# Shared experts and routers of two layers: from the half of the batch into each batch's own thread

## The chip, the cores and the metric

The kernel runs on one core of a Trainium2 chip. The metric is the device time of one execution in microseconds (us), lower is better. The core has five engines that run beside each other, each with its own queue of instructions in a fixed order: TensorE (matmuls; PE in the profile, with its weight loads as PEld), VectorE (DVE), ScalarE (ACT), GpSimd (POOL) and SyncE (SP, which here issues the loads by DMA). An instruction waits in its queue for everything that stands ahead of it, and for semaphores set by other engines or by DMAs.

## The reference, cut to what matters

The program is a decoder of four layers on x of shape [4 batches, 256 tokens, 128 features], in fp32. Each layer is three residual steps:

```python
x = x + attention(layernorm(x))
x = x + cross_attention(layernorm(x), context)
x = x + ffn(layernorm(x))
```

Two of the four FFNs are mixtures of experts with one **shared expert** that every token passes. Layer 0 (16 routed experts of 128 hidden features, each token goes to the best one; f is the layer's normalised input):

```python
logits = f @ router_w.T
score  = sigmoid(logits of the best expert)
routed = down[e](up[e](f * score) * silu(gate[e](f * score)))
shared = (silu(f @ shared_gate_w.T) * (f @ shared_up_w.T)) @ shared_down_w.T   # 512 hidden
ffn    = shared + routed
```

Layer 3 (7 routed experts of 512 hidden features, each token goes to the best two; the shared expert has 512 hidden features as well):

```python
probs = softmax(f @ router_w.T)
top_vals, top_idx = top_k(probs, 2)
top_vals = top_vals / (top_vals.sum(-1) + 1e-9)
routed = sum over the two of top_vals * swiglu[e](f)
ffn    = swiglu_shared(f) + routed
```

The other layers have attentions of several kinds. Two of their parts come up below: layer 3's attention over 64 slots of heads (`heads64`), and layer 3's cross-attention step, in which the 16 heads of one token attend to each other (`across_heads`), so that it consists of elementwise products and sums.

## The kernel before, in words

**Tiles of tokens.** The four batches are two halves: half 0 is batches 0 and 1, half 1 is batches 2 and 3. A batch has two tiles of 128 tokens (tokens on partitions), a half four. The residual x, the normalised y and its transpose yT (features on partitions, 512 tokens in the free dimension) are kept in SBUF for each half.

**Threads and a planner.** Every part of the network is a Python generator. It issues instructions until it needs something, and then yields that need: a tile that must be written, a buffer that must be free, a weight that must be in the ring, or a `Side` (a group of threads) that must be done. A planner, `Clock`, keeps an estimated time for every engine, tile and buffer while the program is built, and `Threads.run` always resumes the generator whose needs are met earliest by these estimates. So the order of the instructions in each engine's queue is written out while the program is built, and follows from the planner's estimates and from what waits for what; on the chip nothing is reordered. All engine calls go through one helper (`Timed`), so that nearly every row of the profile has line 480; rows are told apart by the names of their tiles.

**The halves.** `half(hf)` runs once for each half, both as threads beside each other. `part(hf, batches)` makes the generators, once for both batches of a half (n = 4 tiles of tokens) and once for each batch alone (n = 2):

```python
for head, _ in parts: side.start(head())     # per batch
yield side                                   # both batches done
yield from experts0()                        # layer 0's FFN, both batches together
for _, tail in parts: side.start(tail())     # per batch
yield side
yield from experts3()                        # layer 3's FFN
```

`head` is layer 0's attention (`retention`), cross-attention (`cross0`, tiles x0..) and `normalised`, which writes y and yT. `tail` is everything from layer 1 to layer 3's cross-attention: `linear`, `latent`, `experts1` (issued by batch 0 for all batches), `heads16` twice (tiles a2.., x2..), `ternary`, `heads64` (tiles h6..), `across_heads` and `normalised`.

**across_heads** of one batch does four products on GpSimd for the scores (tiles am, each followed by a sum `en<-am` on VectorE), a softmax (mx, exp on ScalarE, sums), four products on GpSimd for the output (tiles aw, summed on VectorE), a layernorm, transposes (azT), one product on TensorE (apo) and the residual sum. Then `normalised` writes y, and yT by the transposes yt on TensorE.

**The mixture FFN.** `experts0` and `experts3` work on a half's 512 tokens:

- `shared_expert(name)` loops over four groups of 128 hidden features: `gate_up` issues two matmuls of 512 columns (tile gu, gate and up), ScalarE copies the gate and takes a tanh, VectorE makes h in two steps; then a down matmul adds to `acc`. `add_half` scales `acc` on ScalarE, transposes it back (fT, four transposes) and adds it to x. In the trace a matmul in fp32 leaves two records.
- `routes0` and `routes3` are the routers: four small matmuls (lg, lg3), a chain of small VectorE instructions for the best experts and their weights (max, max_index for each tile), and then `dispatch`.
- `dispatch` compares each token's expert with 0, 1, 2, ... (tile mine), counts by two matmuls (rank), and works out on VectorE the place of every token in tiles of 128 tokens of one expert (room, count, end, place, and as integers placei). GpSimd then scatters the rows of y to these places in DRAM (an indirect DMA for each tile and choice: four in layer 0, eight in layer 3). At last the expert of each tile (ids) goes to `ring.numbers`, from which SyncE reads the addresses of the weights to load.
- `routed` loads the sorted tokens back (xs), transposes them (xsT, xT), and goes over 19 tiles in layer 0 (four to a step) or 14 in layer 3, with gate_up (gu, h), a product (eo), a scaled copy (eos) and a store to DRAM (results).
- `collected` gathers each token's rows from the results by indirect DMAs on GpSimd (tile got), and they are added to x.

In `experts0` the shared expert `L0F4` runs beside the router. In `experts3` the shared expert `L3F7` of half 0 runs beside its router, ahead of the routed tiles; that of half 1 is started after its routed tiles, beside the gathers of the results.

**The ring of weights.** `Ring` holds the weights of each half in three slots (`SLOTS`), filled by SyncE in one fixed order. The next name is loaded once the name three places ahead of it was given up by `ring.done`. In half 1 the order ends with the 14 routed weights L3G0 to L3G13 and then L3F7; five of the 14 have two slots of their own (tile late).

**What sets the order around the change.** Both halves share TensorE's PSUM buffers and all engines. Half 0 runs ahead; while GpSimd works on the `across_heads` of half 0, TensorE works on half 1's `heads64`, and so on. `h6p` is the softmax's scaling in `heads64`, on GpSimd.

## The time and the profile before

| | |
|---|---|
| median of 3 runs | 1201.03 us (1199.13 to 1206.34) |
| profiled execution | 1190.56 us, of which the profile's span is 1188.5 us |
| mean granted TensorE clock | 0.811 of full speed |
| instructions | 15677 |
| TensorE busy (PE) | 918.7 us, 77% of the span |
| weight loads (PEld) | 613.5 us, 52% |
| VectorE busy | 756.1 us, 64% |
| ScalarE busy | 385.7 us, 32% |
| GpSimd busy | 385.0 us, 32% |
| moved by DMA | 73.52 MB, 62 GB/s over the span |

How to read the lines that are shown below. The profile is of one execution. In the slices, each digit is the busy share of one of 40 equal parts of the span (29.7 us each) in tenths, 9 being 90% or more; PEclk is the granted TensorE clock in the same way. A row "by stretch" gives for a window of time each engine's busy time with the number of instructions in brackets, and then the granted clock, the busy share of the DMA engines and what they moved. A line of the chain of waits gives the start in us from the span's start, the duration in us, the engine, and the output tile, with the inputs behind an arrow; "x4" means that four instructions of one kind were folded into the line. The chain is followed back from the last instruction, at each step to what released it.

Where the stages of the end lie in this execution: `across_heads` of half 0 from 836 to 920 us, the routed tiles of half 0 and `heads64` of half 1 from 920 to 1025, `across_heads` of half 1 from 1025 to 1085, then its router, its dispatch, and its routed tiles from 1125 on.

### The profile page before, as it was taken

To read this page: it belongs to the slowest core of one execution; us is meant where nothing else is said; L and a number is where in the kernel's file an instruction comes from. 1 tells how busy PE (TensorE), PEld (TensorE's weight loads), DVE (VectorE), ACT (ScalarE), POOL (GpSimd) and SP (SyncE) were. 2 spreads that over 40 slices of the span, in tenths; PEclk is the share of its full clock that TensorE was granted. 3 is DMA by queue.
4 is the path that set the end of the run, shared out by engine and by line. 5 is a ranking of instruction groups with operands and counts; after the bars stand their busy time and mean duration, and the time that the engine had idled before them with its cause. 6 is when DMAs were issued, how large, how long until landed. Compare 5 with 4: busy or idle time off the path is not lost.

```text
span 1188.5 us, 15677 instructions
## 1 busy us (share of the span) xinstructions
PE 918.7 (77%) x5605; PEld 613.5 (52%) x5606; DVE 756.1 (64%) x1836; ACT 385.7 (32%) x870; POOL 385.0 (32%) x493
## 2 busy tenths in 40 slices
PE   2887978996776768999998879997278999732296
PEld 1654544573464446665655445655144567721194
DVE  4547547445785697566578658756877655675154
ACT  0222522352132122224562717363033354210043
POOL 3533031002224310133100535223866422574202
PEclk9989978697888675558795859999678999965599
DMA  9210100441523000001000210011000224411572
GB/s 302 70 55 5 37 1 18 113 127 36 175 65 109 28 0 28 1 1 52 1 1 6 73 45 1 1 46 54 18 1 1 71 77 141 147 35 27 182 235 89
DMA packets 43069, 73.52 MB, mean 62 GB/s; under 512 B 3696, under 2 KB 33008, under 8 KB 42992
## 3 DMA queue, kind: packets, MB, share of 16 engines
q1 hardware_dynamic: 31600, 61.90, 16.3%
q0 software_dynamic: 2560, 6.30, 1.7%
q10 hardware_dynamic: 8832, 4.33, 1.2%
q8 instruction: 44, 0.72, 0.3%
q14 instruction: 33, 0.27, 0.1%
HBM read 63.60 MB, written 8.91 MB: 61 GB/s over the span
## 4 chain that ended last, share of the span: by engine, by line
PE 55%; DVE 20%; POOL 12%; issue 5%; ACT 4%; DMA 3%; another core or an unknown queue 0%; SPq 0%; POOLq 0%; DVEq 0%; ACTq 0%
PE gu L480 7%; PE pj_b L480 6%; DVE mx_b L480 3%; POOL aw_b L480 3%; PE h6av_b L480 3%; PE lc_b L480 3%; POOL ri_b L480 3%; PE h6pt_b L480 2%; PE h6sc_b L480 2%; PE a2sa_b L480 2%; PE eo L480 2%; PE x2av_b L480 2%; PE x0av_b L480 2%; PE a2sb_b L480 2%; PE a2av_b L480 2%
## 5 line engine op out<-in xcount | busy, mean ns | idle before, releaser
L480 POOL TENSOR_TENSOR ri_b<-ri_b,mhalf 128x2 f32<-128x2 f32 (+2 forms) x69 | 58.0, 843 | 243.3 <-DVE ri_b L480 236.3
L480 POOL TENSOR_SCALAR h6p_b<-h6p_b,rec_b 128x256 f32<-128x256 f32 x128 | 59.3, 483 | 117.1 <-DVE rec_b L480 96.5
L480 ACT ACTIVATE h6p_b<-h6sc_b,nm_b 128x256 f32<-128x256 f32 x128 | 59.0, 475 | 56.4 <-DVE nm_b L480 54.0
L480 ACT COPY h<-gu 128x512 f32<-128x512 f32 (+1 forms) x54 | 31.4, 581 | 101.2 <-PE gu L480 101.0
L480 DVE TENSOR_TENSOR h<-h,gu 128x512 f32<-128x512 f32 (+1 forms) x54 | 36.6, 677 | 34.1 <-ACT sl L480 32.9
L480 POOL TENSOR_SCALAR_AFFINE_SELECT a2p_b<-a2p_b 128x256 f32<-128x256 f32 x64 | 27.2, 449 | 81.4 <-ACT a2p_b L480 81.4
L480 ACT COPY yT<-yt_b 128x256 f32<-128x256 f32 x31 | 11.5, 372 | 125.2 <-PE yt_b L480 125.2
L480 PE MATMUL lc_b<-w_L1X,luT 96*128 96x384 f32 x96 | 49.1, 648 | 2.9 <-DVE lpr_b L480 2.4
L480 PE MATMUL gu<-xT,w_L3G 128*128 128x128 f32 x368 | 49.9, 291 | 1.8 <-DMA w_L3G<-in_L3G_dram 1.5
L480 PE MATMUL h6pt_b<-ident,h6p_b 128*128 128x128 f32 x256 | 41.4, 288 | 10.3 <-POOL h6p_b L480 3.8
L480 PEld LDWEIGHTS gu<-xT,w_L3G 128*128 128x128 f32 x368 | 46.6, 204 | 4.9 <-issue 2.5
L480 POOL DMA_INDIRECT got<-results,placei x24 | 23.9, 994 | 77.9 <-PE gu L480 57.2
L480 POOL TENSOR_TENSOR aw_b<-en_b,as_b 128x1024 f32<-128x1024 f32 x16 | 45.5, 2876 | 8.7 <-DVE en_b L480 8.7
L480 PE MATMUL h6sc_b<-hkt_b,hqt_b 64*128 64x256 f32 x256 | 47.8, 434 | 0.1
L480 PE MATMUL yt_b<-ident,y 128*128 128x128 f32 x82 | 23.0, 366 | 31.7 <-DVE y L480 17.8
L480 DVE TENSOR_REDUCE mx_b<-x0sa_b 128x4 f32<-128x1024 f32 x32 | 38.7, 1220 | 12.7 <-PE x0sa_b L480 8.2
L480 PE MATMUL h6av_b<-h6pT_b,hv_b 128*64 128x256 f32 x256 | 46.0, 398 | 0.7 <-DVE h6pT_b L480 0.4
L480 DVE TENSOR_REDUCE nm_b<-h6sc_b 128x4 f32<-128x1024 f32 x32 | 38.9, 1217 | 10.2 <-PE h6sc_b L480 10.0
L480 DVE TENSOR_REDUCE mx_b<-x2sa_b 128x4 f32<-128x1024 f32 x32 | 38.8, 1218 | 8.1 <-PE x2sa_b L480 7.3
L480 PEld LDWEIGHTS h6pt_b<-ident,h6p_b 128*128 128x128 f32 x256 | 28.8, 144 | 27.0 <-issue 6.8
L480 POOL DMA_INDIRECT places<-y,placei x24 | 23.5, 979 | 58.1 <-DVE placei L480 52.0
L480 PE MATMUL a2sa_b<-a2k_b,a2q_b 32*128 32x256 f32 (+1 forms) x128 | 30.0, 458 | 13.7 <-DVE mx_b L480 11.4
(460 smaller groups left out, 2523.5 us busy)
## 6 DMA issues: line engine op xcount, KB each, us to landing
w_L3G<-in_L3G_dram SPq DMA_DIRECT2D x23, 768.0 KB, 6.3
w_L0G<-in_L0G_dram SPq DMA_DIRECT2D x38, 192.0 KB, 2.4
late<-in_L3G_dram SPq DMA_DIRECT2D x5, 768.0 KB, 4.7
xs<-places SPq DMA_DIRECT2D x6, 512.0 KB, 4.1
places<-ones SPq DMA_DIRECT2D x2, 1216.0 KB
results<-eos ACTq DMA_DIRECT2D x8, 256.0 KB, 4.1
results<-eos ACTq DMA_DIRECT2D x14, 128.0 KB, 3.0
w_L2A<-in_L2A_dram SPq DMA_DIRECT2D x2, 776.0 KB
```

The costliest lines, as they stand in the source:

```text
L480: return getattr(self.engine, op)(*args, **kw)
```

## The change

Each batch's thread now computes its own shared expert and its own router. A batch's `head` ends with the router `routes0` and the shared expert `L0F4`, its `tail` with `routes3` and `L3F7`. The two batches of a half share a `Routes` object, which holds the chosen experts (and in layer 3 the weights) of all four tiles and counts the batches that have written theirs. `experts0` and `experts3` of the half are left with the dispatch, the routed tiles, the gathers and the sum. They wait for the `Routes` to be complete and not for the batches' threads; `half` runs them ahead of `yield side`, so a shared expert may still be at work while the dispatch goes on.

In `shared_expert` a batch has 256 tokens: two calls of `gate_up`, each with two groups of 128 hidden features side by side (four matmuls of 256 columns, h again 512 wide), then the four down matmuls into an `acc` of 256 columns, the scaled copy, two transposes and the sum into x. The slot of the ring is given up when both batches are done. In half 1's ring L3F7 now stands ahead of L3G0. The final store of x moves from `experts3` to `half`.

```diff
     rings = [
         Ring(0, first_half + ["L3F7"] + routed3, []),
-        Ring(1, ["L1K"] + [n for n in first_half if n not in alone] + routed3 + ["L3F7"], [n for i, n in enumerate(routed3) if i % 5 > 2]),
+        Ring(1, ["L1K"] + [n for n in first_half if n not in alone] + ["L3F7"] + routed3, [n for i, n in enumerate(routed3) if i % 5 > 2]),
     ]
...
+    class Routes:
+        def __init__(self, name, experts, weights=None):
+            self.experts, self.done = const.tile(experts, F32, tag=f"{name}e", name=f"{name}e"), 0
+            if weights is not None:
+                self.weights = const.tile(weights, F32, tag=f"{name}w", name=f"{name}w")
+
+        def ready(self):
+            return clock.ready(self.experts) if self.done == 2 else math.inf
+
+    routing = [
+        {"L0G": Routes(f"L0G{hf}", [P, 4]), "L3G": Routes(f"L3G{hf}", [P, 2, 4], [P, 2, 4])} for hf in range(2)
+    ]
...
         def shared_expert(name):
-            yield ring.there(name), av_free
+            yield ring.there(name)
             w = ring[name]
-            acc = av_tile("acc")
             hs = []
...
-            for i in range(4):
+            for i in range(2):
                 yield sc_free, t2_free, h_free(i)
-                hs.append(gate_up(i, [(w["g"][:, i, :], w["u"][:, i, :], yT)]))
-                if i > 1:
-                    yield hs[i - 2][1]
-                    product(i - 2)
-            for i in (2, 3):
-                yield hs[i][1]
-                product(i)
-            ring.done(name)
-            yield from add_half(acc)
+                hs.append(gate_up(i, [(w["g"][:, j, :], w["u"][:, j, :], yT) for j in (2 * i, 2 * i + 1)]))
+            yield hs[0][1]
+            yield hs[1][1], av_free
+            acc = av_tile("acc", (P, S))
+            for j in range(4):
+                h = hs[j // 2][0][:, j % 2 * S : j % 2 * S + S]
+                pe.matmul(acc, w["d"][:, j, :], h, start=(j == 0), stop=(j == 3))
+            for h, _ in hs:
+                release(h)
+            ring.done(name, users=2)
+            yield t2_free
+            o = t2("fo", (P, S))
+            nc.scalar.mul(o, acc, 0.5)
+            yield o, ps_free
+            add(transposed(o.rearrange("p (t q) -> p t q", q=P), n, "fT").rearrange("p (t q) -> p t q", q=P))
...
         def experts0():
...
-            got = []
-            side.start(routes0(got))
-            yield from shared_expert("L0F4")
-            yield side
+            yield routes["L0G"].ready
+            placei = yield from dispatch("L0G", routes["L0G"].experts, 16, 16, TILES0)
             yield from routed("L0G", TILES0, 4, 1)
             yield results[hf]
-            t = collected(got[0])
+            t = collected(placei)
...
-        def routes0(got):
+        def routes0():
             yield ps_free
-            pl = ps("lg", (P, 4, 16))
-            for t in range(4):
+            pl = ps("lg", (P, n, 16))
+            for t in range(n):
                 pe.matmul(pl[:, t, :], yT[:, t * P : (t + 1) * P], wM["r0"], start=True, stop=True)
...
+            routes["L0G"].done += 1
...
         def experts3():
-            got = []
-            side.start(routes3(got))
-            if hf == 0:
-                yield from shared_expert("L3F7")
-            yield side
+            yield routes["L3G"].ready
+            experts, tv = routes["L3G"].experts, routes["L3G"].weights
+            placei = yield from dispatch("L3G", experts.rearrange("p j t -> p (j t)"), 8, 7, TILES3)
             yield from routed("L3G", TILES3, 1, 1 + hf)
-            if hf == 1:
-                side.start(shared_expert("L3F7"))
             yield results[hf]
-            t = collected(got[1])
+            t = collected(placei)
...
-            yield side
-            nc.sync.dma_start(out[2 * hf : 2 * hf + 2].rearrange("b (c p) d -> p (b c) d", p=P), x)
...
         def head():
...
             yield from cross0()
             yield from normalised()
+            side.start(routes0())
+            yield from shared_expert("L0F4")
+            yield side
 
         def tail():
...
             yield from across_heads()
             yield from normalised()
+            side.start(routes3())
+            yield from shared_expert("L3F7")
+            yield side
...
         for head, _ in parts:
             side.start(head())
+        yield from experts0()
         yield side
-        yield from experts0()
         for _, tail in parts:
             side.start(tail())
+        yield from experts3()
         yield side
-        yield from experts3()
+        nc.sync.dma_start(out[2 * hf : 2 * hf + 2].rearrange("b (c p) d -> p (b c) d", p=P), xs[hf])
```

`routes3` is changed as `routes0` is: n tiles in place of four, the chosen experts and their weights written to the `Routes`, and the weights now worked out before `dispatch` rather than after it.

## The prediction

> **What bounds the kernel now.** I read the page's slices first, then busy time by stretch, then the chain at the end.
>
> ```profile
> span 1188.5 us, 15677 instructions
> PE   2887978996776768999998879997278999732296
> POOL 3533031002224310133100535223866422574202
> PEclk9989978697888675558795859999678999965599
> ```
>
> TensorE is eight or nine tenths busy nearly everywhere and falls off in a few places: slices 10 to 15, slice 29 (832 to 862 us), and slices 36 to 38 (1040 to 1129 us), where half 1 is alone. The stretches of layer 3:
>
> ```profile
> core 0: us, PE busy (x) PEld busy (x) DVE busy (x) ACT busy (x) POOL busy (x), PEclk, DMA share, GB/s
> 836.00:920.00 84.00, 50.58 (x206) 28.96 (x206) 67.48 (x122) 21.82 (x68) 62.61 (x52) 0.72 0.02 7
> 920.00:1025.00 105.00, 100.52 (x669) 73.84 (x668) 62.56 (x148) 46.46 (x135) 30.82 (x55) 0.98 0.34 108
> 1025.00:1085.00 60.00, 19.05 (x124) 17.76 (x124) 41.76 (x53) 6.43 (x13) 51.02 (x25) 0.65 0.17 54
> 1098.00:1105.00 7.00, 1.31 (x6) 1.06 (x6) 4.93 (x38) 0.23 (x1) 0.00 (x1) 0.50 0.00 0
> 1105.00:1125.00 20.00, 1.68 (x8) 1.57 (x8) 0.00 (x0) 0.50 (x1) 7.77 (x8) 0.50 0.76 269
> ```
>
> 836 to 920 is `across_heads` of half 0 (GpSimd 62.6 of 84 us). From 920 to 1025 TensorE is the bound, 100.5 of 105 us: `heads64` of half 1 and routed tiles of half 0. From 1025 to 1085 GpSimd is the bound: `across_heads` of half 1. Then come half 1's router (1098 to 1105) and the transfers of its dispatch (1105 to 1125), with TensorE almost idle. The end, from the chain of waits:
>
> ```profile
> 1098.05 1.04 PE lg L480 x4
> ...
> 1113.95 5.00 DMA places<-y,placei
> 1119.10 4.09 DMA xs<-places
> 1123.32 1.94 PE xsT L480 x8
> ...
> 1162.36 4.48 DMA w_L3F<-in_L3F_dram
> ...
> 1181.48 0.70 DVE x L480
> 1183.00 0.99 DVE x L480 x4
> ```
>
> The chain names half 1's shared expert from 1162 to 1181. The timeline warns: its eight gathers of results run on GpSimd from 1172.12 to 1182.43, and in half 0 each `x<-got` started 1.6 us after its gather's instruction ended, so the last `x<-got` (1184.0) comes when the gathers allow, with or without the shared expert. Removing it from the end is worth little.
>
> **The change part by part.** Durations are of this execution: 1188.5 us of span, 2.1 us around it, 1190.56 together. The median of the runs shown is 1201.03, 0.88% above; I carry the result over as a ratio. Where instructions stand I take from the two programs' built orders.
>
> *The split itself.* A half's shared expert is 12 matmuls of 512 columns; now each batch has 12 of 256. In the chain four 512-column records (a matmul leaves two) take 1.73 us, 0.43 each; the timeline's 256-column `pj_b` records come 0.215 apart. So the split costs TensorE 0. The Trainium skill speaks against it: "TensorE: Matmul & The Clock Gate", section "Why this matters for your kernels", asks for all dimensions of 512 or more, and its "Back-to-back issue gap" gives sustained 81 ns at 128 columns and 131 ns at 512. Between these, an estimate of 98 ns at 256 would make two halves cost 1.5 times one whole: of a half's 10.3 us, 5.2 more, four times, so +20.6 us of TensorE work. The row decides: these fp32 records cost in proportion to columns, I take 0. VectorE and ScalarE write as many elements of h as before; the doubled routers add some 57 small VectorE instructions of 0.1 to 0.2 us, under VectorE's 36% idle time except where counted below. Ends 0 and +2.
>
> *Layer 0.* Batch 0's shared expert (12 x 0.43 = 5.2 us) now stands ahead of batch 1's last matmuls of `cross0`, on a TensorE busy 39.3 of 43 us (185 to 228), so half 0's dispatch comes later. In return batch 2's stands between half 0's last `eo` and batch 3's `x0po`, just before the hole at 268.2 to 276.9 where TensorE waits 8.7 us for half 0's gathers and layernorm. What is late next there is batch 3's own shared expert and half 1's dispatch. I take 0; ends -8.7 (the hole filled) and +7 (the later dispatch passed on).
>
> *Half 0 goes ahead in layer 3.* The new order runs half 0's 16 products of `across_heads` on GpSimd with none of half 1's `h6p` between, and half 0's dispatch with three pairs of heads less of half 1 done. So half 1 falls back against half 0. Before, when half 1's first `ak_b` stood in TensorE's queue, half 0 still had 32 `gu` and 20 `eo` matmuls and two transposes to come, which ran under GpSimd's products. After, 8 `eo` remain. So 44 matmuls and two transposes move from under the 1025 to 1085 stretch to before it. In the chain 16 `gu` records take 1.79 us and 8 `eo` 0.89: 0.224 a matmul, 9.9, and 0.25 for the transposes: **+10.1**. They go where TensorE has no room. I assume that TensorE's other idle time before half 1's `across_heads` stays as it was; ends -6 (half 0's stage gets shorter by more than the work taken out of it) and +15.
>
> *Half 1's `across_heads`.* Eight `am_b` took 19.7 us, six `aw_b` 17.4: 2.47 and 2.90 each. Half 0's gathers (9.9 us) move from between the last `aw_b` to after the fifth `am_b`. Now: five `am_b` 12.3, gathers to 22.2, batch 2's last `am_b` to 24.7, its reduction 1.2 and softmax 4.4 (1046.2 to 1050.6 in the trace) to 30.3, while the other two `am_b` end at 29.6; eight `aw_b` to 53.5. Before it was 1084.25 - 1025.24 = 59.0. The gap of 5.7 us before `aw_b` closes: **-5.5**. From the last `aw_b` to yT it took 13.7 us, since `x<-got` and `az_b` of batch 2 held VectorE; the instructions alone with 0.1 us between them make 11.3: **-2.4**. Ends of the two: -11 and -2.
>
> *Half 1's dispatch.* Before, the router's matmuls followed the last transpose, `mine` was 4.0 us after yT, `placei` 6.7 us. Now TensorE's queue holds between batch 3's transposes and `rank`: 8 `gu` of batch 2, the 4 router matmuls, 8 `gu` of batch 3, all 4 `acc` of batch 2, 2 `acc` of batch 3. TensorE comes from idle at half clock; in the timeline a burst after such idle took 4.91 us for 30 records instead of 3.66, so 1.3 us more. Eight `gu` 3.4 + 1.3 = 4.7; router 0.5; four `gu` 1.7, at 6.9; ScalarE's copy of them 0.6 and then batch 3's exp 0.2, which is queued behind it, 7.9 with handovers. VectorE then does two router chains of 2.2 us each (s to `mine` took that for four tiles) and, queued between, three h instructions of 0.69: `mine` at about 14.5, against 4.0. `rank`, behind two `acc` that wait for batch 3's h, follows at once. From there on `placei` is queued behind `x<-fT` of batch 3 (0.4). Behind `placei` wait the eight scatters on GpSimd, then xs on SP, then all routed tiles. **+11.0**; ends +5 (chains overlap) and +19 (22 matmuls of 256 columns all at 0.86 us).
>
> *The end.* After the last tile nothing of the shared expert is left. It delayed the last `eo` (h ready 1166.93, end 1168.96): **-0.9**. Its late load, 4.48 us in the chain, is hidden by the gathers anyway; now it waits for `hpv` of half 1 on SP, ahead of half 0's tile 9, whose load waits for a later matmul. Ends -2 and 0.
>
> Sum: 10.1 - 5.5 - 2.4 + 11.0 - 0.9 = +12.3. 1190.56 + 12.3 = 1202.9, a ratio of 1.0103; on 1201.03 that is **1213.4 us**. About 1% (12 us) is what a measurement of this kernel can tell from no change.
>
> **The rivals.**
>
> *Faster: idle time ahead of half 1 closes.* Before 1025 us TensorE is idle 187 us (1025 - 687.0 before 836 - 50.6 - 100.5), of which 33.4 in 836 to 920 and 43.6 in 185 to 396, where the joins stand. These 77 us are what a batch that need not wait could fill. For it speaks that half 0's GpSimd stage loses `h6p` and so about 17 us. Against it: the 12.7 us of heads that ran beneath it leave too. It decides from 12.3 us on; a third of the 77, 26 us, gives -13.7: 1187 us. Chance 0.15.
>
> *No difference: the moved tiles find room.* If the 10.1 us fall into idle time and the rest stays, +2.2 remains: 1203 us. For it: slices 30 and 31 (862 to 921 us) are only seven and eight tenths busy. Against: 100.5 of 105. Chance 0.18.
>
> *Clearly slower: half clock in the dispatch.* Waits between the shared experts keep TensorE cold: +19 instead of +11, and layer 0 gives +7: +27, 1228 us. For it: clock 0.50 from 1085 to 1125. Against: a burst of 16 `gu` is longer than what warmed it at 1125. Chance 0.20.
>
> *The change doesn't do what it says:* half 1's dispatch waits on TensorE for both batches' shared experts, so the halves join later than the router's end. That is in my forecast, not beside it.
>
> **How the numbers follow.** The forecast has 0.47, its own range 1205 to 1222, lying on the 1% line: 0.30 of it slower, 0.17 within. With the rivals: slower 0.30 + 0.20 = 0.50, within 1% 0.17 + 0.18 = 0.35, faster 0.15. The range for 8 in 10 reaches from 1190, most of the way to the faster case, to 1230.
>
> **What would show it.** Right: half 1's first `am_b` about 10 us later; from there to its last `aw_b` some 53 us, not 59; from yT of batch 3 to `placei` some 17 us, not 6.7; after the last `eo` the same 15 us. Wrong: the first `am_b` at 1025 or earlier (then TensorE's idle time fell), or `mine` within 6 us of yT.

## The result and the profile after

The changed kernel takes 1211.91 us in the median of 4 runs (1209.3 to 1222.35), the kernel before 1200.08 in the median of its 4 (1197.18 to 1206.34). The ratio is **1.0138, with a 95% interval from 1.0098 to 1.0178**. Timed again later beside other kernels it was 1.0108 (1.0069 to 1.0147). So the change costs a little over 1%. The forecast was a ratio of 1.0103 and 1213.4 us, on the right side and near the size.

The profiled execution of the changed kernel took 1214.11 us, with a span of 1212.4. The slices of its page, in the rows shown of before:

```profile
span 1212.4 us, 15934 instructions
...
PE   3879997988786868988999589995159999503393
...
POOL 3641121011226111241003523225852522574202
PEclk9967987797795865667976679998569999855697
```

TensorE's low place in the middle has become deeper and longer: slices 28 to 30 read 5, 1 and 5, where before they read 7, 2 and 7. Slices 35 to 37 now read 5, 0 and 3, so while GpSimd works on half 1's `across_heads` TensorE has almost nothing left.

The next view gives busy time by stretch for the changed kernel: engines with the number of instructions, then clock, DMA share and GB/s. The cuts are events: half 0's first `am`, half 1's first `am`, yT of batch 3 written, `placei` of half 1, the last `eo`, the end.

```profile
core 0: us, PE busy (x) PEld busy (x) DVE busy (x) ACT busy (x) POOL busy (x), PEclk, DMA share, GB/s
837.80:1045.50 207.70, 154.85 (x1004) 116.94 (x1005) 143.37 (x304) 70.56 (x208) 92.52 (x105) 0.85 0.23 73
1045.50:1115.50 70.00, 8.26 (x39) 6.49 (x39) 40.31 (x71) 2.02 (x4) 51.22 (x28) 0.55 0.05 13
1115.50:1130.20 14.70, 12.67 (x59) 10.05 (x58) 10.51 (x58) 5.42 (x12) 0.00 (x0) 0.95 0.00 0
1130.20:1193.10 62.90, 42.87 (x350) 41.80 (x350) 21.13 (x31) 17.67 (x36) 7.80 (x8) 0.81 0.62 212
1193.10:1212.40 19.30, 0.00 (x0) 0.00 (x0) 2.81 (x8) 0.37 (x1) 7.63 (x8) 0.57 0.17 48
```

The table sets the same stretches beside each other. Both programs were profiled twice (`before_again` and `after_again` below are the same two kernels once more); all values are us.

| stretch | before, two profiles | after, two profiles | difference of the means |
|---|---|---|---|
| start to half 0's first `am` | 836.7, 841.3 | 837.8, 833.3 | -3.4 |
| to half 1's first `am` | 188.5, 184.1 | 207.7, 207.7 | **+21.4** |
| to yT of batch 3 | 72.8, 72.8 | 70.0, 70.0 | -2.8 |
| to `placei` of half 1 | 6.7, 6.7 | 14.7, 14.7 | **+8.0** |
| to the last `eo` | 64.3, 63.0 | 62.9, 63.1 | -0.7 |
| to the end | 19.5, 19.6 | 19.3, 19.3 | -0.2 |
| span | 1188.5, 1187.5 | 1212.4, 1208.1 | +22.2 |

The profiles show 22 us, the timed ratios 13 to 17 us. The two profiled executions of before (1190.56 and 1189.49 us) were quick ones: they lie 9.5 and 3.1 us under the medians of the runs timed with them (1200.08 and 1192.61). That is the larger part of what lies between. Profiled executions can lie further from their medians (10.7 us under it for `l3_only` below, 8.7 for `l0_half0`), so profiles are compared here by stretches.

**Where the 21 us come from.** TensorE's busy time in the stretch between the two first `am` rose by 5 us (154.85 and 154.88 against 151.10 and 148.00), its idle time by 16. The timeline on TensorE shows most of it as one gap; the last column is the idle time ahead of the instruction and what ended it. The changed kernel:

```profile
842.08 0.71 PE L480 MATMUL av_b<-w_L3X,ctxT 128*128 128x128 f32 x4
872.54 0.61 PE L480 MATMUL bp_b<-ident,qi_b 128*128 128x128 bf16 x4 [29.74 <-DVE qi_b L480]
```

In the kernel before, the gap ahead of the same matmul was 9.78 us:

```profile
855.16 0.61 PE L480 MATMUL bp_b<-ident,qi_b 128*128 128x128 bf16 x4 [9.78 <-DVE am_b L480]
```

`qi` and `bp` belong to half 1's `ternary`, whose second layernorm takes its root (`ri`) and its scale and shift (`bqt`, four products) on GpSimd. GpSimd's timeline of the changed kernel:

```profile
837.77 18.35 POOL L480 TENSOR_TENSOR am_b<-as_b 128x1024 f32<-128x1024 f32 x8 [1.76 <-DVE as_b L480]
856.09 1.17 POOL L480 TENSOR_TENSOR ri_b<-ri_b,mhalf 128x1 f32<-128x1 f32 x2
857.30 1.26 POOL L480 TENSOR_TENSOR bqt_b<-bqt_b,w_L2F 128x512 f32<-128x512 f32 x1
858.92 4.16 POOL L480 TENSOR_TENSOR bqt_b<-bqt_b,w_L2F 128x512 f32<-128x512 f32 x3 [0.36 <-DVE bqt_b L480]
```

And of the kernel before:

```profile
836.68 2.35 POOL L480 TENSOR_TENSOR am_b<-as_b 128x1024 f32<-128x1024 f32 x1
839.00 0.73 POOL L480 TENSOR_TENSOR ri_b<-ri_b,mhalf 128x1 f32<-128x1 f32 x1
839.71 2.33 POOL L480 TENSOR_TENSOR am_b<-as_b 128x1024 f32<-128x1024 f32 x1
842.00 5.11 POOL L480 TENSOR_TENSOR bqt_b<-bqt_b,w_L2F 128x512 f32<-128x512 f32 x4
...
847.74 14.31 POOL L480 TENSOR_TENSOR am_b<-as_b 128x1024 f32<-128x1024 f32 x6
```

Before, `bqt` stood behind two of half 0's eight `am` products of 2.3 us each. Now it stands behind all eight. From half 0's first `am` to this `bp` it is 34.8 us instead of 18.5, and while half 1 is not ready TensorE has nothing else: half 0 is on GpSimd too. This is the largest cost of the change, and it lies in a part of the network that the diff does not touch.

The place in the queue is not what most of these 16 us were spent on. The same `ternary` passes ScalarE (tile bv) shortly ahead of its layernorm. First the kernel before, then the changed one:

```profile
829.81 1.06 ACT L480 ACTIVATE bv_b<-bkt_b 128x1024 f32<-128x1024 f32 x1 [6.56 <-DVE bkt_b L480]
```

```profile
844.35 1.06 ACT L480 ACTIVATE bv_b<-bkt_b 128x1024 f32<-128x1024 f32 x1 [6.87 <-DVE bkt_b L480]
```

Before, `bv` starts 6.9 us ahead of half 0's first `am` (6.7 in the second profile), now 6.6 us behind it in both profiles. So half 1's last batch had already lost 13.3 us against half 0 when it came to this queue. From `bv` to `bp` it takes 28.2 us instead of 25.2: the longer queue added 3.0 to that way. From `bp` to half 1's first `am` it takes 172.9 us in both profiles, before 170.1 and 165.6. The 21.4 us are thus 13.3 of lag on arrival, 3.0 between `bv` and `bp`, and 5.1 behind `bp`, where TensorE's busy time rose by 5.0.

The lag comes in between 684 and 844 us. From the end of the last batch's first `heads16` on GpSimd (the last `a2p`) to its `bv` it takes 160.7 and 160.8 us, before 145.7 and 145.2, while half 0 takes 154.1 and 154.2 from that moment to its first `am`, before 152.5 and 151.9. In that time the batch's second `heads16` shares TensorE with half 0's `heads64`: when its last `x2av` matmul ends, half 0 has 60 of its `h6p` behind it, before 52. Why an edit in layer 0 leads to this order was not traced.

**Where the 8 us come from.** TensorE in the changed kernel, from half 1's last transposes to the dispatch's `rank`:

```profile
1113.69 1.07 PE L480 MATMUL gu_b<-yT,w_L3F 128*128 128x256 f32 x2
1114.56 0.42 PE L480 MATMUL yt_b<-ident,y 128*128 128x128 f32 x1
1114.77 4.34 PE L480 MATMUL gu_b<-yT,w_L3F 128*128 128x256 f32 x14
1118.95 0.95 PE L480 MATMUL lg_b<-w_M,yT 128*128 128x7 f32 x8
1119.76 1.97 PE L480 MATMUL gu_b<-yT,w_L3F 128*128 128x256 f32 x8
...
1126.95 0.19 PE L480 MATMUL rank<-mine,earlier 128*128 128x64 bf16 x1
```

The router's matmuls (`lg`) follow the whole of batch 2's gate and up, and `rank` comes 7 us after the last `lg` has ended. Before, it was 3 us:

```profile
1098.05 1.02 PE L480 MATMUL lg<-w_M,yT 128*128 128x7 f32 x4 [0.46 <-ACT yT L480]
1102.05 0.24 PE L480 MATMUL rank<-mine,earlier 128*128 128x64 bf16 x1 [2.97 <-DVE mine L480]
```

The granted clock of the changed kernel in this stretch is 0.95: 0.50 up to 1117.0 us, the first 1.6 us of it, and 1.00 from 1119 on.

### The profile page after: what moved, and what is told of

It is laid out like the page before. It is cut to its first block, busy times and chain, and to the rows that moved or that the text cites. A ratio compares the mean times of both kernels' runs of the same rounds, so it can differ in the third digit from the quotient of the medians.

```text
span 1212.4 us, 15934 instructions
## 1 busy us (share of the span) xinstructions
PE 917.5 (76%) x5702; PEld 631.1 (52%) x5702; DVE 764.7 (63%) x1875; ACT 381.2 (31%) x871; POOL 384.4 (32%) x493
## 4 chain that ended last, share of the span: by engine, by line
PE 47%; DVE 21%; POOL 13%; issue 11%; ACT 4%; DMA 4%; POOLq 0%; SPq 0%; ACTq 0%; DVEq 0%
PE gu L480 5%; PE pj_b L480 4%; PE h6av_b L480 3%; POOL ri_b L480 3%; POOL am_b L480 3%; PE gu_b L480 3%; PE eo L480 2%; PE lc_b L480 2%; POOL aw_b L480 2%; DVE mx_b L480 2%; PE h6sc_b L480 2%; PE h6pt_b L480 2%; PE x0av_b L480 2%; POOL got L480 2%; PE a2av_b L480 2%
## 5 line engine op out<-in xcount | busy, mean ns | idle before, releaser
L480 POOL TENSOR_TENSOR ri_b<-ri_b,mhalf 128x2 f32<-128x2 f32 (+2 forms) x69 | 58.0, 845 | 272.2 <-DVE ri_b L480 229.5
L480 POOL TENSOR_SCALAR h6p_b<-h6p_b,rec_b 128x256 f32<-128x256 f32 x128 | 59.8, 487 | 151.5 <-DVE rec_b L480 148.1
L480 DVE TENSOR_SCALAR y<-x,mv_b,ri_b 128x128 f32<-128x128 f32 x90 | 31.8, 386 | 26.3 <-POOL ri_b L480 26.1
L480 DVE TENSOR_REDUCE nm_b<-h6sc_b 128x4 f32<-128x1024 f32 x32 | 39.0, 1221 | 11.8 <-PE h6sc_b L480 11.3
L480 PE MATMUL h6sc_b<-hkt_b,hqt_b 64*128 64x256 f32 x256 | 43.2, 410 | 3.1 <-ACT h6p_b L480 3.0
L480 DVE COPY h6pT_b<-h6pt_b 128x512 f32<-128x512 f32 x53 | 35.2, 683 | 16.0 <-PE h6pt_b L480 13.8
L480 DVE TENSOR_TENSOR h<-h,gu 128x512 f32<-128x512 f32 (+1 forms) x38 | 25.7, 676 | 26.8 <-ACT sl L480 26.3
L480 ACT COPY h<-gu 128x512 f32<-128x512 f32 (+1 forms) x38 | 22.1, 581 | 64.4 <-PE gu L480 64.2
L480 ACT ACTIVATE x2p_b<-x2sb_b 128x1024 f32<-128x1024 f32 x32 | 32.8, 1026 | 29.2 <-PE x2sb_b L480 28.3
```

The lines of the kernel that those rows point to most:

```text
L480: return getattr(self.engine, op)(*args, **kw)
```

## The experiments

All ratios are to the kernel before, of runs on the same chip, with the 95% interval. Stretches are read from the profile of each run as in the table above. The built order of a program tells where each instruction stands in its engine's queue, without times. "Joined" functions are those of the kernel before, kept under new names (`experts0_joint`, `experts3_joint`) beside those of the change.

### A second profile of each

**before_again** is the kernel before, unchanged.

> The kernel before, unchanged, for a second profile of it: the first one (1190.56 us) lay 0.8% below the median of its runs, so part of the 24 us between the two profiles may be one execution against another. If so, this one ends at 1197 to 1203 us, and half 1's first am_b stands at 1030 to 1038 us rather than at 1025. If the profile is typical, first am_b stands at 1025 and the sum of the whole change has to be explained from 24 us.

Measured: the profiled execution took 1189.49 us, and half 1's first `am` stands at 1025.4, against 1025.2 in the first profile. So the first profile was no stray, and the 24 us between the spans of the first two profiles had to be explained. From half 1's first `am` on, the two profiles agree within 1.3 us in each stretch.

**after_again** is the changed kernel, unchanged.

> The changed kernel, unchanged, timed beside the same runs of the kernel before as the parts of it, and profiled a second time. If the parts add up (layer 0 alone 1.0116, layer 3 alone 1.0066), the ratio is 1.014 to 1.019. If layer 3's cost is partly hidden behind layer 0's, it is 1.011 to 1.014. The stretches of the profile: first am of half 0 to first am of half 1 206 to 210 us, yT to placei of half 1 14 to 15.5 us.

Measured: 1.0108 (1.0069 to 1.0147), first `am` to first `am` 207.7 us, yT to `placei` 14.7. The ratio is under what the parts below add up to (1.0116 times 1.0066 is 1.0183). Both intervals of the whole and those of the parts are wide enough for either reading, so the times leave open whether layer 3's cost is partly hidden. The profiles speak for adding up: from half 0's first `am` to the end, l0_only takes 19.4 us more than the mean of the two profiles of before, l3_only 3.4, and the changed kernel 25.7.

### Which layer costs what

**l0_only**: layer 0 as changed, layer 3 as before. Edit against the changed kernel (half 1's ring as before too):

```diff
-            side.start(routes3())
-            yield from shared_expert("L3F7")
-            yield side
...
-        yield from experts3()
         yield side
+        yield from experts3_joint()
```

> Layer 0 as in the changed kernel (shared expert and router in each batch's thread), layer 3 as before. In the built order half 0 then stands as far ahead of half 1 at half 1's across_heads as in the changed kernel: 8 eo of half 0 are left there, against 32 gu and 20 eo before. Theory: the lead of half 0 comes from layer 0 and costs what stands before half 1's first am_b: 8 to 12 us slower than before (ratio 1.007 to 1.010), with yT to placei of half 1 at 6.7 us as before. Rival, as the prediction placed it: layer 0 costs nothing, everything comes from layer 3: ratio 0.997 to 1.003.

Measured: **1.0116 (1.0069 to 1.0163)**. First `am` to first `am` 208.5 us, the gap ahead of `bp` 29.8, yT to `placei` 6.7. The theory holds in its place: the lead of half 0 and the gap behind it come from layer 0, where the prediction had put nothing. `bv` stands 6.6 us behind half 0's first `am`, as in the changed kernel. The time lies a little above the expected 1.007 to 1.010, which the interval covers.

**l3_only**: layer 3 as changed, layer 0 as before:

```diff
-            side.start(routes0())
-            yield from shared_expert("L0F4")
-            yield side
...
-        yield from experts0()
         yield side
+        yield from experts0_joint()
```

> Layer 3 as in the changed kernel, layer 0 as before. The built order keeps 32 gu and 20 eo of half 0 under half 1's across_heads, and has the shared experts ahead of rank as in the changed kernel. Theory: only the dispatch of half 1 is paid, yT to placei 14 to 15 us instead of 6.7, less 1.3 at the end: 6 to 8 us slower than before (ratio 1.005 to 1.007). Rival, as the prediction placed it: layer 3 also brings the lead of half 0, first am_b 10 us later, and the whole of the change is here: ratio 1.010 to 1.014.

Measured: **1.0066 (1.0038 to 1.0094)**. By stretch, from half 0's first `am`:

```profile
834.70:1019.50 184.80, 150.29 (x900) 107.22 (x901) 132.35 (x282) 66.68 (x203) 92.61 (x105) 0.87 0.21 69
1019.50:1090.50 71.00, 22.95 (x140) 20.12 (x139) 48.18 (x80) 6.79 (x14) 52.76 (x28) 0.65 0.15 50
1090.50:1105.40 14.90, 12.94 (x59) 10.26 (x58) 10.50 (x59) 5.42 (x12) 0.00 (x0) 0.93 0.00 0
```

The first stretch is as long as before (184.8), and TensorE still has 23 us of matmuls under half 1's `across_heads`. Only the third is longer, 14.9 instead of 6.7. So layer 3's part costs its dispatch and nothing else of size.

**l0_half0** and **l0_half1**: layer 0 as changed for one half only, everything else as before; `head` ends with the router and the shared expert for that half alone.

```diff
-        yield from experts0()
-        yield side
+        if hf == 1:                      # l0_half1: hf == 0
+            yield side
+            yield from experts0_joint()
+        else:
+            yield from experts0()
+            yield side
```

> Layer 0's shared expert and router in each batch's thread for half 0 only; the rest as before. In the built order half 1's four bqt products of ternary (GpSimd) stand behind the second of half 0's am products, as before, and 32 gu and 20 eo of half 0 are left at half 1's across_heads. Theory (half 0's lead over half 1 at that place is the cost): same time as before, ratio 0.997 to 1.003, first am of half 0 to first am of half 1 184 to 189 us. Rival (the split or the doubled routers of layer 0 cost): half of what layer 0 alone cost, 1.005 to 1.007.

> Layer 0's shared expert and router in each batch's thread for half 1 only; the rest as before. In the built order half 1's ternary rsqrt and bqt products stand behind seven and eight of half 0's am products, as in the changed kernel, and nothing of half 0's routed tiles is left at half 1's across_heads. Theory: as layer 0 alone or more, ratio 1.010 to 1.018, first am of half 0 to first am of half 1 205 us or more, with a TensorE gap of about 30 us behind half 0's am. Rival: half of layer 0's cost, 1.005 to 1.007.

Measured: half 0 alone **0.9943 (0.9912 to 0.9975)**, half 1 alone **1.0188 (1.0141 to 1.0235)**. Half 0's part is even a small gain, outside both expectations, though its interval touches the theory's range. From first `am` to first `am` it takes 184.3 us, as before. Half 0's first `am` stands at 828.2 us, before at 836.7 and 841.3, but this profiled execution was 8.7 us quicker than its median, and I did not trace the gain to one place. Half 1's part takes 221.2 us there, with a gap of 28.5 us ahead of `bp`, and on GpSimd seven `am` ahead of the first `ri` and all eight ahead of `bqt`; the stretch from half 1's first `am` to yT, which no longer holds half 0's gathers, gives 11 us back (61.5). So the cost of layer 0 comes from **half 1** having its shared experts in its threads, and in both kernels that have this alone or with half 0's, its `bqt` is queued behind half 0's eight `am`. The lag goes with it: `bv` stands 4.6 us behind half 0's first `am` in l0_half1, and 6.8 ahead of it in l0_half0.

### Is it the queue on GpSimd?

**after_dve**: the changed kernel with half 1's second layernorm of `ternary` off GpSimd, for both of its batches.

```diff
-            nc.gpsimd.tensor_tensor(o, o, mhalf.to_broadcast(list(var.shape)), ALU.pow)
+            if dve:                      # only this layernorm, half 1
+                nc.scalar.activation(o, o, AF.Sqrt)
+                nc.vector.reciprocal(o, o)
+            else:
+                nc.gpsimd.tensor_tensor(o, o, mhalf.to_broadcast(list(var.shape)), ALU.pow)
...
-                nc.gpsimd.tensor_tensor(z[:, 0, :], z[:, 0, :], w2["ln2_w"], ALU.mult)
-                nc.gpsimd.tensor_tensor(z[:, 0, :], z[:, 0, :], w2["ln2_b"], ALU.add)
+                e = nc.vector if hf == 1 else nc.gpsimd
+                e.tensor_tensor(z[:, 0, :], z[:, 0, :], w2["ln2_w"], ALU.mult)
+                e.tensor_tensor(z[:, 0, :], z[:, 0, :], w2["ln2_b"], ALU.add)
```

> The changed kernel, but for half 1 the second layernorm of ternary takes its root on ScalarE and its reciprocal on VectorE, and its two products run on VectorE, not on GpSimd, so that they are not queued behind half 0's eight am. Theory: the 29.7 us gap of TensorE behind half 0's am shrinks to some 10 to 15 us, and from half 0's first am to half 1's it takes 185 to 195 us instead of 207.7; 12 to 20 us faster than the changed kernel, ratio to before 0.995 to 1.004. Rival: the gap is filled but the work only moves (TensorE is as late at half 1's am): 1.010 to 1.014.

Measured: **1.0044 (1.0016 to 1.0073)**. First `am` to first `am` takes 196.0 us instead of 207.7, and the gap ahead of `bp` 21.1 instead of 29.7. The direction is the theory's and the rival's 1.010 is outside the interval, but the gap shrank less than expected. The lag is still there, with `bv` 6.6 us behind half 0's first `am`. VectorE's timeline shows a further part of the reason:

```profile
850.70 0.14 DVE L480 TENSOR_SCALAR ri_b<-mv_b 128x1 f32<-128x1 f32 x1
851.85 1.22 DVE L480 TENSOR_REDUCE en_b<-am_b 128x128 f32<-128x1024 f32 x1 [1.01 <-POOL am_b L480]
852.99 0.21 DVE L480 RECIPROCAL ri_b<-ri_b 128x1 f32<-128x1 f32 x2
...
854.77 2.49 DVE L480 TENSOR_TENSOR bqt_b<-bqt_b,w_L2F 128x512 f32<-128x512 f32 x4
```

On VectorE the sums `en<-am` stand in the queue between `ternary`'s instructions, and each sum waits for its `am` on GpSimd. The queue of one engine had been left for that of another that is paced by the first.

The run shows that this layernorm on GpSimd lies in the path. It does not measure what the change had put there. From `bv` to `bp` it takes 19.6 us here, 28.2 in the changed kernel, and 25.2 in the kernel before, so the edit removes more than the change had added; the same edit in the kernel before was not run. And some 4 of the 8.6 us are not of the queue. In the changed kernel the last two instructions ahead of `bp` ran on VectorE while GpSimd was at its `aw` products, first there and then here:

```profile
867.22 2.35 DVE L480 TENSOR_SCALAR bqt_b<-bqt_b,sx_b 128x512 f32<-128x512 f32 x1
869.76 2.72 DVE L480 TENSOR_SCALAR qi_b<-bqt_b 128x512 bf16<-128x512 f32 x1
```

```profile
860.41 0.48 DVE L480 TENSOR_SCALAR bqt_b<-bqt_b,sx_b 128x512 f32<-128x512 f32 x1
861.39 0.42 DVE L480 TENSOR_SCALAR qi_b<-bqt_b 128x512 bf16<-128x512 f32 x1
```

The two long ones each ended 0.28 us after a product on GpSimd had ended (at 869.30 and 872.20). In after_dve GpSimd had no work at that time.

### The shared expert ahead of the dispatch

**late_shared**: the changed kernel, with half 1's shared experts of layer 3 started when the dispatch is issued.

```diff
             side.start(routes3())
+            if hf == 1:
+                yield lambda: 0.0 if routes["L3G"].done == 3 else math.inf
             yield from shared_expert("L3F7")
...
             placei = yield from dispatch("L3G", experts.rearrange("p j t -> p (j t)"), 8, 7, TILES3)
+            routes["L3G"].done = 3
```

> The changed kernel, but in layer 3 half 1's shared experts are started only after the dispatch is issued, so that 10 gu matmuls of 256 columns stand ahead of rank and not 16 gu and 6 acc, and no h of theirs ahead of the routers on VectorE. Theory: yT to placei falls from 14.7 us to 8 to 11 and the rest of the shared experts runs while the scattered tokens are loaded back (TensorE is idle there for 15 us): 4 to 6 us faster than the changed kernel, ratio to before 1.006 to 1.010. Rival: the wait is not in the path (the transfers end as late as before): same time as the changed kernel, 1.012 to 1.014.

Measured: **1.0101 (1.0070 to 1.0131)**. yT to `placei` takes 9.2 us instead of 14.7, and from there to the last `eo` 59.8 instead of 62.9: together 8.6 us less, of which 0.8 is given back ahead of yT (70.8). The timed ratio is 0.0037 (4.4 us) under the first one of the changed kernel and 0.0007 under the second, so no gain in time can be told from none. The stretches are clear of doubt, since they repeat to 0.2 us in the changed kernel's two profiles. `gu` matmuls of the shared experts still stand ahead of `rank` (22 records in its trace), though their thread starts behind it: so a step behind the threads still moves instructions in the queues, and the threads and their planner alone do not fix the order, as the section on the kernel has it.

### The price of the split

**split_only**: the kernel before, with gate and up of the shared experts as two matmuls of 256 columns each.

```diff
-                hs.append(gate_up(i, [(w["g"][:, i, :], w["u"][:, i, :], yT)]))
+                hs.append(gate_up(i, [(w["g"][:, i, :], w["u"][:, i, :], yT[:, c : c + S]) for c in (0, S)]))
```

> The kernel before, with each gate or up matmul of the shared experts (512 columns) issued as two of 256 columns: 32 more matmuls in all, the order of everything else as before. By the row of the trace before (0.43 us per record of 512 columns, 0.215 per record of 256) it costs nothing: ratio 0.998 to 1.002. [...]two thirds of 20.6 us, 13.7 us of TensorE, of which the two shared experts of the busy stretches would show: 1.005 to 1.011.

Measured: **0.9895 (0.9859 to 0.9931)**: 1% faster, which neither expected. The groups by form, of the kernel before and then of this one (count, busy us, mean ns), for layer 3's shared expert:

```profile
L480 PE MATMUL gu<-yT,w_L3F 128*128 128x512 f32 x32 | 15.4, 598 | 1.0 <-DMA w_L3F<-in_L3F_dram 0.8 <-DVE h L480 0.2
```

```profile
L480 PE MATMUL gu<-yT,w_L3F 128*128 128x256 f32 x64 | 15.5, 382 | 1.0 <-DMA w_L3F<-in_L3F_dram 0.9 <-DVE h L480 0.2
```

Twice as many records of half the columns take 15.5 us instead of 15.4. The split costs nothing here, as the prediction took it; the estimate that it was weighed against would have had 1.5 times as much. The expectation was wrong that the rest of the order stays: the planner sees other durations, and layer 0 has another order. Before, TensorE stood still for 8.69 us there, ahead of half 1's first `yt` after half 0's gathers (8.46 in the second profile). In this kernel the longest gap at that place is 3.48 us:

```profile
270.08 1.20 PE L480 MATMUL x0po_b<-w_L0X,x0of_b 128*128 128x128 f32 x4 [3.48 <-DVE lcols L480]
```

Half 0's first `am` then stands at 830.4 us, 6 to 11 earlier than in the profiles of before, and the stretches behind it are as before (185.1, 73.8 and 6.7 us). That the shorter gap is what won the time is not shown: half 1's first `yt` behind it starts at 272.2 us, in the profiles of before at 276.9 and 271.5.

### Versions that are faster than both

**split_late**, **split_h0** and **split_h0_late** put together the parts that had gained, in time or only in their stretches: the joined shared experts with matmuls of 256 columns (as in split_only), half 0 of layer 0 in each batch's thread (as in l0_half0), and half 1 of layer 3 as in late_shared. Against the changed kernel, split_h0_late has these edits; split_h0 has the first and third and layer 3 joined for both halves, split_late the second and third and layer 0 joined for both halves.

```diff
         def head():
...
-            side.start(routes0())
-            yield from shared_expert("L0F4")
-            yield side
+            if hf == 0:                  # 1: half 1 runs experts0_joint behind both heads
+                side.start(routes0())
+                yield from shared_expert("L0F4")
+                yield side
...
         def tail():
...
-            side.start(routes3())
-            yield from shared_expert("L3F7")
-            yield side
+            if hf == 1:                  # 2: half 0 runs experts3_joint behind both tails
+                side.start(routes3())
+                yield lambda: 0.0 if routes["L3G"].done == 3 else math.inf
+                yield from shared_expert("L3F7")
+                yield side
...
         def shared_joint(name):
...
-                hs.append(gate_up(i, [(w["g"][:, i, :], w["u"][:, i, :], yT)]))
+                hs.append(gate_up(i, [(w["g"][:, i, :], w["u"][:, i, :], yT[:, c : c + S]) for c in (0, S)]))   # 3
```

> Layer 0 and half 0 of layer 3 as before but with the gate and up matmuls of the shared experts split into 256 columns (as in split_only); half 1 of layer 3 as in late_shared: router and shared expert in each batch's thread, the shared expert not before the dispatch is issued. In the built order bqt stands behind two am and half 0 has 32 gu and 20 eo left, as before. Theory: the gain of split_only (it closed the 8.7 us TensorE gap of layer 0), and in half 1 of layer 3 the dispatch costs 2.5 us more but the way from the first am to yT is 1.7 and from placei to the last eo 3 us shorter: ratio 0.985 to 0.990. Rival: half 1's part brings nothing: 0.989 to 0.993.

> Layer 0 of half 0 in each batch's thread as in the change; all other shared experts joined as before, with gate and up matmuls of 256 columns. In the built order bqt stands behind two am, and half 0 has 56 gu and 32 eo left at half 1's across_heads (before: 32 and 20). Theory (the smaller half 0's lead, the more of its matmuls run under half 1's am and aw): half 1's first am comes 36 matmuls, 8 us, earlier after half 0's than in split_only, 175 to 180 us, and what is moved is hidden: ratio 0.982 to 0.989. Rival: half 0's routed tiles now end too late, and its gathers hold up half 1: 0.990 to 1.000.

> Both together: layer 0 of half 0 in each batch's thread, half 1 of layer 3 as in late_shared, the joined shared experts with matmuls of 256 columns. By the first theories of the two it is the fastest, 0.979 to 0.987; by their rivals 0.990 to 1.000.

| kernel | ratio | to half 0's `am` | to half 1's `am` | to yT | to `placei` | to the last `eo` |
|---|---|---|---|---|---|---|
| split_late | 0.9919 (0.9887 to 0.9951) | 832.9 | 190.1 | 73.2 | 6.8 | 59.3 |
| split_h0 | 0.9764 (0.9711 to 0.9818) | 824.1 | 177.3 | 68.1 | 6.7 | 63.8 |
| split_h0_late | **0.9687 (0.9640 to 0.9735)** | 822.0 | 177.6 | 71.2 | 9.3 | 59.0 |

split_late gave its rival's ratio: it has its 4 us ahead of the last `eo` against split_only, and 5 us more between the two first `am`, where the two profiles of before also differ by 4.4 us. split_h0 hit its stretch (177.3 of the expected 175 to 180) and was better in time than its theory. What it has beyond it lies ahead of half 0's first `am` (824.1 against 830.4) and on the way to yT (68.1 against 73.8); its profiled execution was 5.6 us quicker than its median. The kernel with all three, also under its theory's range, has 1160.98 us in the median beside 1199.04 for before: 3.1% faster, and 4% faster than the changed kernel in the same runs (1209.83). Its stretches:

```profile
822.00:999.60 177.60, 142.42 (x829) 98.32 (x829) 127.49 (x266) 63.33 (x194) 93.00 (x105) 0.87 0.18 59
999.60:1070.80 71.20, 36.35 (x203) 33.25 (x202) 52.67 (x85) 11.02 (x22) 53.76 (x28) 0.70 0.23 76
```

TensorE does 36 us of matmuls in the stretch of half 1's `across_heads` (the second row), where the kernel before did 25 and 23 and the changed kernel 8. In the built order 56 `gu` and 32 `eo` of half 0 are left there, against 32 and 20 before and none and 8 in the changed kernel. This is the reverse of the changed kernel: more of half 0's routed tiles are left to run while GpSimd holds half 1. The lag of `ternary` is not what differs here (`bv` 7.1 us ahead of half 0's first `am`, before 6.9 and 6.7). The gain lies behind it: from `bp` to half 1's first `am` it takes 159.2 us, before 170.1 and 165.6. What each of the three edits brings in this kernel was not separated further.

## Why the prediction was right, and where it was not

The total was right, at 1.0103 against 1.0138 and 1.0108, and partly by luck. The sum was made on a profile, +12.3 us, and between the profiles the change is 22 us. Its two large errors, 11.3 us for half 0's lead and 5.1 for half 1's `across_heads` and the way to yT, both put it too low, and the dispatch and the time up to half 0's first `am` took back only 3.0 and 3.4. It came near the timed ratios because the profiled executions of before were quicker than their medians. Point by point:

- **The split, 0.** Right: 15.5 against 15.4 us.
- **Layer 0, 0 with ends of -8.7 and +7.** For the time up to half 0's first `am` this holds (-3.4, less than two executions of one kernel differ by). But the term was drawn too narrowly: layer 0 sets how far half 0 is ahead 500 us later, and l0_only shows all of that cost.
- **Half 0 goes ahead in layer 3, +10.1.** This step failed, in its place and its size. The lead comes from layer 0, and of it from half 1's part (l0_half1 1.0188, l0_half0 0.9943, l3_only's first stretch as before). The size was 21.4 us, outside the ends of -6 and +15. That half 1 falls back against half 0 was right, and the matmuls that move are there, with about half the forecast size (5.1 us behind `bp`). The assumption that failed is the sentence that TensorE's other idle time stays as it was: 16 us of idle time came in, because half 1's last batch came to its `ternary` 13.3 us later against half 0, and 3.0 us because its `bqt` then stood behind eight `am` instead of two. The built order, which I had used to count TensorE's matmuls, shows that position on GpSimd too.
- **Half 1's `across_heads` and the way to yT, -5.5 and -2.4.** Together -2.8 instead of -7.9. With half 0's gathers now among the `am`, VectorE's sums `x<-got` came between batch 2's last `en` and its softmax. On VectorE:

```profile
1069.39 1.22 DVE L480 TENSOR_REDUCE en_b<-am_b 128x128 f32<-128x1024 f32 x1 [2.90 <-POOL am_b L480]
1070.53 3.80 DVE L480 SCALAR_TENSOR_TENSOR x<-got,L3G0w,x 128x128 f32<-128x128 f32 x2
1074.26 0.67 DVE L480 TENSOR_REDUCE amx_b<-en_b 128x32 f32<-128x512 f32 x1
```

  The first of the two `x<-got` took 3.54 us, the others of this kind 0.35. It did not wait for its gather, since GpSimd had issued the last one by 1067.0 and the line shows no idle time; it ran beside GpSimd's last `am` products and ended 0.16 us after the last of them (1073.91). The kernel before has the same: an `az` took 5.50 us instead of 0.34 and ended 0.09 us after an `aw`. The sums `en`, 1.2 us, take as long beside a product as without one. The gap ahead of the `aw` is 6.54 us, before it was 5.69, so it did not close. That an instruction on VectorE can take this much longer beside a product on GpSimd stood in no term of the sum.
- **Half 1's dispatch, +11.0.** The mechanism was right and the size a little high: +8.0, `mine` 11.1 us after yT and not 14.5. The first eight `gu` and the router's matmuls had ended 4.4 us after yT, where the sum had 5.2, since the first of them ran before batch 3's yT was written. The larger part is VectorE: the sum had put the two batches' router chains behind each other, 2.2 us each; the trace has them interleaved, from the sums to the chosen experts in 2.5 us (1122.56 to 1125.05) with an h instruction among them.
- **The end, -0.9.** Right: -0.7 and -0.2.
- **The rivals.** The faster one needed TensorE's idle time ahead of half 1 to close; it opened. No difference needed room for the moved matmuls; the stretch became 21 us longer. The half clock did not last through the dispatch: 0.50 was granted up to 1117.0 us, 1.6 us after yT, and 1.00 from 1119 on. That is the cold burst of 1.3 us that the forecast itself had.

## What to carry to other kernels

When a change shifts two interleaved streams against each other, follow every queue they share at the places where one stream holds an engine for long, not only the engine that bounds the kernel. Here 13 us of lag left TensorE without work while GpSimd was at eight long products, and put a short product behind all of them; together this cost more than everything in the diff. Measure both apart: the lag on arrival, and what the queue adds (here 3 us). Moving such a product to another engine helps less if that engine's queue is paced by the first, and an experiment that does so needs its twin in the kernel before. And where a planner sets the order, any edit is also an edit of the order elsewhere: parts of this change, put together with matmuls split in two, were worth 3% in the other direction.

## What the runs showed that I had not expected

Two executions of one program repeat very well in the last stretches and not in the long first one: from half 1's first `am` to yT 72.8 and 72.8 us, 70.0 and 70.0, yT to `placei` the same to 0.1, but up to half 0's first `am` 836.7 and 841.3, or 837.8 and 833.3. Between the two first `am` the changed kernel repeats (207.7 twice, at a granted clock of 0.85 both times) and the kernel before does not (188.5 and 184.1, at 0.86 and 0.88). What sets the difference was not tested. So a difference of 4 us could be read in the last 170 us of one pair of profiles, and not in the first 840.
